# Moving the start of one filler stream in a hand-woven order: the last layer of group 6 of a four-layer graph network

## The chip, the cores and the metric

The kernel runs on one core of one Trainium2 chip. The metric is the device time of one execution in microseconds (us), from a few runs; a profile of one further execution is used to see where the time goes.

## What is computed

Thirty-two graphs `x` of 512 nodes with 256 features share one sparse 512 x 512 matrix `adj`. Four layers follow each other. Layers 0 and 3 have the same form and their own weights:

```python
pre_u = h_t @ W1[:d];  pre_v = h_t @ W1[d:]
hidden = relu(pre_u[:, :, None, :] + pre_v[:, None, :, :] + b1)
S   = sigmoid(hidden @ W2 + b2)                    # one number for each pair u, v
a_t = einsum('buv,bud->bvd', S * A_a, h_t)
m_t = einsum('uv,bud->bvd', A_m, h_t) * h_t
z_t = beta1*h_t + beta2*(a_t @ Wa + ba) + beta3*(m_t @ Wm + bm)
```

`A_a` and `A_m` are both `adj`. Layer 1 is `z + relu((adj @ z) @ W.T + b)`. Layer 2 is an attention: a softmax over `leaky_relu(f1_i + f1_j) + adj`, applied to `x @ W1.T`, plus the input. All is float32.

## The kernel before, in words

**Sparse edges.** `S` is needed only where `adj` is not zero. The kernel first turns `adj` into 36 lists of 128 edges, called items (32 for the first eight neighbours of each node, 4 for the rest). The graphs are worked on in eight groups, 0 to 7, of four entries (graphs) each. For each group and for each of layers 0 and 3, `pre` (L560) computes `pre_u` and `pre_v` of every node and writes them to a table in DRAM (`table<-puv`, L577). `edges` (L606) then goes through the 36 items. GpSimd (POOL) gathers the 128 rows of 4 KB at the other ends of the edges (L602), VectorE (DVE) adds the own rows (`mine`, L674), and relu, times W2 and a sum follow. In the last group's edges of layer 3 that is one DVE instruction of 128x1024 (L680) and four of ScalarE (ACT, L685); elsewhere it is four of DVE (L687). Every four items the sigmoid is finished (L587, L591, L592, L631). The results are put into a dense array `cells` in DRAM by an indirect write of POOL (L596). When all puts are done, `load` (L706) reads `cells` back as `SA`, four tiles of 128x2048.

**Stages.** Each group passes through these streams, each a Python generator that yields after every piece:

- `first` and `edges` of layer 0: table and edge values;
- `middle` (L773, L810): for each of the four entries, the end of layer 0, layers 1 and 2, and at the end the `pre` of layer 3. The lines that matter here are WT (L45 `WT,hT`), `adjT,zW`, L852, the projection `WT,yT`, L870, the softmax on DVE and ACT (L878 to L884), its transposes (L923) with ACT's copy `eT` (L924), the product `eT,feats`, L901, the product `w_L_gnn_W,yT` of `pre`, and the transposes L912;
- `edges` of layer 3;
- `last` (L987): the end of layer 3. For each of its four entries there are eight pieces: two of `hWa` (L45 `L_gnn_Wa,hT` with ACT's copy L725), two of `mhT` (L45 `adj,h` with DVE's product L735), two that open the sums over `SA` (L972, preceded by DVE's L965), and two that close them (L981, then DVE's L984). The output of an entry leaves by a DMA on SyncE (SP, L998 or L1007) once the next entry's `hWa` is recorded. Then the next `h` (L928) is loaded, and after `mhT` the next `hT` (L933).

The last group has no group behind it. Its last layer is cut in two: `last_before` computes `hWa` and `mhT` during the edges, and `last_behind` does the sums (L972, L981) and the outputs (L956) at the very end.

**Order.** `weave` (L444) orders all pieces by planned times in units of one group. A stream of kind "main" (the middle stages) runs at its own times. Pieces of a "fill" stream (`first` and `last`) fall due at their times; while a main stream runs up to eight (`HELD`) are held back, and one or two of them run where a main piece yields a true value, which marks places where TensorE (PE) would otherwise wait:

```python
if kind == "fill":
    due.append((k, j))
    fill(HELD if running else 0)
...
if room and due:
    fill(len(due) - (1 if len(due) < HELD // 2 else 2))
```

The times are set in `sparse_path`. For group t, `end` is the planned end of its middle stage; `last` of group t has 33 pieces, spread evenly over `behind`. For t = 6, `end` is 6.53. The middle stage of group 7 is planned from 6.53 to 7.33, its edges from 7.333 to 7.79, and `last_before` from 7.62. The framework then schedules the recorded instructions, each engine's in one fixed order, and inserts the waits. On each engine instructions run in that order; SP starts DMAs in its order too.

Of the kernel before, what the change touches and what calls it, by code (L numbers as in the profile page):

```python
# [1009 lines left out]
def even(n):  # L1010
    return [1.0] * n
# [6 lines left out]
def spread(shares, a, b):  # L1018

    times, at = [], 0.0  # L1020
    for share in shares:
        times.append(a + (b - a) * at / sum(shares))
        at += share
    return times


def edge_times(ahead, a, b, behind, lead=LEAD):

    step = (b - a) / ITEMS
    first = [ahead + j * min(step, (a - ahead) / lead) for j in range(lead)]  # L1030
    return first + spread(even(ITEMS), a, b) + spread(even(TAIL), b, behind)


def middle_shares(given):


    hWa = [] if given else [1.7, 1.7]
    shares = list(hWa)
    for b in range(NB):
        more = hWa if b < NB - 1 else []  # L1040
        shares += [] if given else [2.8, 2.8]
        shares += [3.4, 3.4, 1.0, 2.7]
        shares += [1.7, 3.4, 2.8, 4.5] + [0.9] * NC
        shares += [0.4, 0.4, 0.4, 1.0, 0.4, 1.0] + more + [1.5, 1.5]
        shares += [2.8, 4.5] + [0.4] * NC + [0.5, 0.5]
    return shares + [0.1]


@with_exitstack
def sparse_path(ctx, m, counts, xr, outr, B):  # L1050


    sp = Sparse(ctx, m, counts, xr, outr, B)
    last = B // NB - 1
    streams = [
        (sp.setup(), spread(even(NC + 1 + NC + 2 * (OWN // 2 + 1) + 1), -0.40, -0.295), ""),
        (sp.setup_behind(), spread(even(2 * (OWN // 2 + 1) + 2 * PANELS + 4), -0.285, -0.16), ""),
        (sp.setup_rest(), spread(even(7), -0.26, -0.20), ""),
        (sp.zeros_behind(), spread(even(2), 0.15, 0.2), ""),
    ]  # L1060
    for t in range(last + 1):
        g0, g3 = Group(sp, m.g0, f"0_{t}"), Group(sp, m.g3, f"3_{t}")
        start, end = (max(0.0, k - 0.47) for k in (t, t + 1))

        if t == 0:
            first = spread(FIRST, -0.385, -0.30)
            edges0 = edge_times(-0.292, -0.27, -0.03, -0.02, LEAD_AT_ENDS)
        elif t == 1:
            first = spread(FIRST, -0.28, -0.06)
            edges0 = edge_times(0.02, 0.07, start - 0.06, start - 0.04)  # L1070
        else:
            first = spread(FIRST, start - 0.86, start - 0.6)
            edges0 = edge_times(start - 0.552, start - 0.505, start - 0.06, start - 0.04)
        edges3 = edge_times(end + 0.003, end + 0.05, end + 0.48, end + 0.54)
        behind = end + 0.56, end + 1.13
        if t == last - 1:
            edges3 = edge_times(end + 0.003, end + 0.05, end + 0.46, end + 0.5)
            behind = end + 0.6, end + 1.08
        if t == last:
            end -= 0.2  # L1080
            edges3 = edge_times(end + 0.003, end + 0.02, end + 0.45, end + 0.46, LEAD_AT_ENDS)
            behind = end + 0.29, end + 0.45
        streams += [
            (sp.first(g0, t * NB), first, "fill"),
            (sp.edges(g0, ("yT", "mhT3") if t == 0 else ()), edges0, ""),
            (sp.middle(g0, g3, t * NB), spread(middle_shares(t == 0), start, end), "main"),
            (sp.edges(g3, ("yT", "h1", "hT1") if t == last else ()), edges3, "free"),
        ]
        if t == 0:
            streams.append((sp.middle_before(g0, 0), spread(AHEAD, -0.15, -0.03), ""))  # L1090
        if t < last:
            streams.append((sp.last(g3, t * NB), spread(LAST, *behind), "fill"))
        else:
            streams.append((sp.last_before(g3, t * NB), spread(AHEAD, *behind), ""))
            streams.append((sp.last_behind(g3, t * NB), spread(BEHIND, end + 0.5, end + 0.6), ""))
    sp.weave(streams)
# [191 lines left out]
@with_exitstack  # L1288
def adj_seq_kernel(ctx: ExitStack, tc: tile.TileContext, a: dict, out: bass.AP):
    nc = tc.nc  # L1290
    x = a["x"]
    B = x.shape[0]
    xr = x.rearrange("b (c p) d -> b p c d", p=P)
    outr = out.rearrange("b (c p) d -> b p c d", p=P)
    m = Model(ctx, tc, a)
    counts = Counts(ctx, m)
    excess = nc.values_load(counts.excess[0:1, 0:1])
    with tc.If(excess > 0) as branch:
        dense_path(m, xr, outr, B)
    with branch.Else():  # L1300
        sparse_path(m, counts, xr, outr, B)
# [32 lines left out]
```

## Time and profile before

| | us |
|---|---|
| median of 3 runs | 3160.87 |
| lowest and highest of them | 3154.97, 3162.56 |
| the profiled execution, its own time | 3165.21 |
| its span, first to last instruction | 3163.5 |
| PE, DVE, ACT, POOL busy in it | 2734.3, 2357.2, 977.2, 1468.5 |
| mean granted TensorE clock | 0.931 of full speed |

The profile is one execution, so times read from it are held against its own 3165.21 first and then against the median. Busy shares are means over the whole span. The change touches only its last 290 us, so the views used below are cut to stretches of that part. Times in them are us from the start of the span. A line such as L45 is a helper that issues most of the matmuls, so these are told apart by their tiles. Each float32 matmul shows as two records.

### The profile page before, as it was taken

The page shows a single profiled execution, that of the slowest core. Times are in us where ns is not written, and L with a number is a line of the kernel's source. Part 1 is how long each engine was busy: PE and PEld are TensorE (multiplying, and loading weights), DVE is VectorE, ACT ScalarE, POOL GpSimd, SP SyncE. Part 2 cuts the span into 40 slices and gives each one's busy share as a digit, 9 for nine tenths or more (in the row PEclk, how much of TensorE's full clock was granted, in tenths as well). Part 3 has the DMA queues.
Part 4 walks back from the last instruction along what each step waited for, and adds up shares of the span by engine and source line. Part 5 has one row for each costly group of instructions (what it writes and reads, how often), then busy time and mean ns, then how long its engine had stood idle before and what let it go on. Part 6 is the DMA issues. An engine that isn't in the chain of part 4 may idle for free. (4 is left out here: it accounts for less than half of the span.)

```text
span 3163.5 us, 32203 instructions
## 1 busy us (share of the span) xinstructions
PE 2734.3 (86%) x8645; PEld 1650.1 (52%) x8646; DVE 2357.2 (75%) x7594; ACT 977.2 (31%) x2309; POOL 1468.5 (46%) x1312
## 2 busy tenths in 40 slices
PE   6357878889998899989998899989998899979947
PEld 3133444446654565445654565545654466545626
DVE  6773777988589875988588785888679885872661
ACT  4453343222233222332232222332222222232440
POOL 1462453656345552546335562555435563450461
PEclk9688889999998999989998999999999899989979
DMA  8874547876667757786667766786567766551653
GB/s 290 289 231 149 167 160 234 260 246 224 210 206 256 226 191 225 232 275 201 227 191 243 244 208 206 230 268 230 184 215 249 257 212 220 178 190 47 217 189 113
DMA packets 302718, 679.38 MB, mean 215 GB/s; under 512 B 52673, under 2 KB 170945, under 8 KB 294337
## 3 DMA queue, kind: packets, MB, share of 16 engines
q0 software_dynamic: 120384, 406.01, 40.7%
q1 hardware_dynamic: 163184, 234.01, 21.9%
q10 hardware_dynamic: 18960, 37.24, 3.1%
q8 instruction: 70, 1.15, 0.1%
q14 instruction: 120, 0.98, 0.1%
HBM read 531.12 MB, written 146.01 MB: 214 GB/s over the span
## 5 line engine op out<-in xcount | busy, mean ns | idle before, releaser
L602 POOL DMA_INDIRECT rows<-table,iv x554 | 631.8, 1140 | 874.6 <-DVE rows L687 211.6
L596 POOL DMA_INDIRECT cells<-s,cell x576 | 671.1, 1165 | 625.7 <-DMA cells<-s,cell 422.4
L674 DVE TENSOR_TENSOR rows<-rows,mine 128x1024 f32<-128x1024 f32 x554 | 669.1, 1217 | 154.6 <-DMA rows<-table,iv 143.0
L687 DVE SCALAR_TENSOR_TENSOR rows<-rows,L_gnn_W2bc 128x256 f32<-128x256 f32 x2016 | 740.9, 418 | 2.1
L45 PE MATMUL pst<-adj,h 128*128 128x512 f32 x1024 | 454.6, 595 | 0.0
L45 PE MATMUL pst<-L_gnn_Wa,hT 128*128 128x256 f32 x1024 | 266.5, 413 | 123.3 <-DMA hT<-xT 53.7
L45 PEld LDWEIGHTS pst<-adj,h 128*128 128x128 f32 x1024 | 193.8, 191 | 219.0 <-issue 215.4
L45 PEld LDWEIGHTS pst<-L_gnn_Wa,hT 128*128 128x128 f32 x1024 | 209.9, 210 | 171.7 <-issue 64.1
L45 PE MATMUL pst<-w_L_gnn_W,hT 128*128 128x512 f32 x512 | 245.2, 617 | 8.4 <-ACT hT L557 6.0
L45 PE MATMUL pst<-WT,hT 128*128 128x256 f32 x512 | 166.8, 486 | 93.3 <-DVE hT L833 92.7
L45 PE MATMUL pst<-eT,feats 128*128 128x512 f32 x512 | 232.0, 607 | 10.6 <-ACT eT L924 10.0
L45 PE MATMUL pst<-w_L_gnn_W,yT 128*128 128x512 f32 x512 | 226.5, 594 | 1.0 <-DVE yT L901 1.0
L45 PE MATMUL pst<-adjT,zW 128*128 128x512 f32 x512 | 224.9, 592 | 0.0
L972 PEld LDWEIGHTS pst<-hWa,SA 128*128 128x128 f32 x896 | 212.8, 328 | 5.7 <-issue 3.3
L972 PE MATMUL pst<-hWa,SA 128*128 128x256 f32 x896 | 215.0, 397 | 0.0
L794 ACT COPY flat<-SA 128x512 f32<-128x512 f32 x128 | 136.9, 1133 | 237.8 <-PE pst L45 173.5
L825 PE MATMUL pst<-flat,hWa 128*128 128x512 f32 x448 | 196.8, 592 | 0.0
L45 PEld LDWEIGHTS pst<-WT,hT 128*128 128x128 f32 x512 | 121.8, 247 | 142.7 <-DVE hT L833 117.2
L923 PE MATMUL pst<-ident,ex 128*128 128x128 f32 x512 | 92.3, 318 | 114.5 <-DVE ex L884 63.6
L570 ACT COPY puv<-pst 128x256 f32<-128x256 f32 x256 | 93.5, 371 | 292.5 <-DVE puv L569 246.3
L569 DVE TENSOR_TENSOR puv<-pst,bc_L_gnn_b 128x256 f32<-128x256 f32 x256 | 104.2, 415 | 87.8 <-DMA table<-puv 48.0
L45 PEld LDWEIGHTS pst<-eT,feats 128*128 128x128 f32 x512 | 96.8, 193 | 127.1 <-issue 109.5
(166 smaller groups left out, 3646.2 us busy)
## 6 DMA issues: line engine op xcount, KB each, us to landing
table<-puv SPq DMA_DIRECT2D x256, 256.0 KB
SA<-cells POOLq DMA_DIRECT2D x64, 1024.0 KB
h<-in_x_dram SPq DMA_DIRECT2D x64, 512.0 KB
mine<-table SPq DMA_DIRECT2D x64, 512.0 KB
hT<-xT SPq DMA_DIRECT2D x36, 512.0 KB
h<-x2s SPq DMA_DIRECT2D x36, 512.0 KB
xT<-hT ACTq DMA_DIRECT2D x32, 512.0 KB
x2T<-yT SPq DMA_DIRECT2D x32, 512.0 KB
```

Source lines behind the costliest of these rows:

```text
L45: nc.tensor.matmul(out, lhsT, rhs, start=(n == 0), stop=(n == len(pairs) - 1))
L569: nc.vector.tensor_tensor(puv[:, 0, :], pp[:, 0:D], w["b1bc"], ALU.add)
L570: nc.scalar.copy(puv[:, 1, :], pp[:, D:])
L596: self.nc.gpsimd.indirect_dma_start(out=g.cells[half], out_offset=bass.IndirectOffsetOnAxis(ap=at, axis=0), in_=s, in_offset=None)
L602: self.nc.gpsimd.indirect_dma_start(out=rows, out_offset=None, in_=g.table, in_offset=bass.IndirectOffsetOnAxis(ap=at, axis=0))
L674: self.behind(nc.vector.tensor_tensor(rows, rows, other, ALU.add))
L687: nc.vector.scalar_tensor_tensor(part, part, 0.0, w["W2bc"], ALU.max, ALU.mult, accum_out=at)
L794: self.nc.scalar.copy(flat[:, r, :], SA[r][:, :, b])
L825: nc.tensor.matmul(pz, hWa[:, r, cs], flat[:, r, :], start=(r == 0), stop=False)
L923: nc.tensor.transpose(pt[:, js], ex[:, js], self.m.ident)
L972: nc.tensor.matmul(pz[:, k * D : (k + 1) * D], SA[r][:, cs, b], hWa[:, r, :], start=(r + k == 0), stop=False)
```

## The change

The window of `last` of group 6 (`t == last - 1`) is made shorter and begins later: from 7.13..7.61 to 7.23..7.59 in the units of the plan.

```diff
         behind = end + 0.56, end + 1.13
         if t == last - 1:
             edges3 = edge_times(end + 0.003, end + 0.05, end + 0.46, end + 0.5)
-            behind = end + 0.6, end + 1.08
+            behind = end + 0.7, end + 1.06
```

No instruction is added or removed. In the order of the plan, pieces 0 to 11 of the 33 ran before the middle stage of group 7 ended, and 12 to 14 directly at its end; now pieces 0 to 6 run before its end, and 7 to 10 directly at it. The later ones follow every 0.0109 units in place of every 0.0145, and all are still recorded before `last_before` starts.

## The prediction

> **What bounds the kernel now.** The clock per core says one core at a mean granted TensorE clock of 0.931, span 3163.5 us. The diff touches one group of eight only, so I cut the end of the run into stretches at the visible events: end of the last middle stage, first gathered row, first wait of VectorE for a row, last item, first final sum. Windows table (columns: length, then busy us and count of PE, PEld, DVE, ACT, POOL, then clock, DMA share, GB/s):
>
> ```profile
> 2876.00:2948.50 72.50, 69.82 (x234) 43.74 (x233) 22.78 (x50) 15.12 (x32) 0.00 (x0) 0.98 0.15 48
> 2948.50:2961.40 12.90, 12.90 (x58) 12.23 (x58) 1.46 (x6) 1.30 (x4) 5.78 (x7) 1.00 0.97 255
> 2961.40:3017.70 56.30, 51.66 (x184) 37.09 (x182) 56.24 (x67) 36.93 (x167) 37.58 (x28) 1.00 0.73 255
> 3017.70:3088.10 70.40, 26.24 (x64) 15.59 (x64) 42.36 (x59) 30.87 (x144) 45.69 (x38) 0.68 0.56 183
> ```
>
> In the first row PE works 69.8 of 72.5 us and POOL nothing: the last middle entry is bound by PE, and no edge can start before its table is written. In the third row DVE never rests (56.24 of 56.30); in the fourth PE is two thirds idle and DVE waits for gathers. So PE work is dear before 2948.5 and cheap after about 2962.
>
> The PE timeline shows what in that first row belongs to the last layer of group 6 (start, length, tiles, number of records, in brackets the idle time before it; each matmul has two records):
>
> ```profile
> 2820.91 3.72 PE L45 MATMUL pst<-WT,hT 128*128 128x256 f32 x16 [0.82 <-DVE hT L833]
> ...
> 2881.07 3.62 PE L45 MATMUL pst<-L_gnn_Wa,hT 128*128 128x256 f32 x16
> ...
> 2887.98 7.03 PE L45 MATMUL pst<-adj,h 128*128 128x512 f32 x16
> ...
> 2901.71 7.61 PE L972 MATMUL pst<-hWa,SA 128*128 128x256 f32 x32
> ...
> 2911.77 1.89 PE L981 MATMUL pst<-L_gnn_Wm,mhT 128*128 128x256 f32 x8
> ...
> 2914.36 1.89 PE L981 MATMUL pst<-L_gnn_Wm,mhT 128*128 128x256 f32 x8
> ...
> 2916.53 3.62 PE L45 MATMUL pst<-L_gnn_Wa,hT 128*128 128x256 f32 x16
> 2921.68 0.66 PE L923 MATMUL pst<-ident,ex 128*128 128x128 f32 x4 [1.54 <-DVE ex L884]
> ...
> 2923.24 5.29 PE L45 MATMUL pst<-adj,h 128*128 128x512 f32 x8
> ...
> 2937.11 3.60 PE L45 MATMUL pst<-adj,h 128*128 128x512 f32 x8
> ```
>
> By the start of the row that follows each, these pieces hold PE for 3.46, 6.87, 7.45, 1.72, 1.73, 3.46, 5.14 and 3.43 us: 33.3 us, from 2881.07 to the end of the middle stage at 2948.3, which I call M. They are entry 0 of that layer whole, and hWa and mhT of entry 1.
>
> Last, the waits in the edges after M, POOL's and then DVE's (engine, tile, line, released by: total us, times, longest):
>
> ```profile
> POOL cells L596 <- DMA cells<-s,cell: 19.5, 8, 5.3
> POOL rows L602 <- ACT rows L685: 7.6, 5, 2.4
> ```
>
> ```profile
> DVE rows L674 <- DMA rows<-table,iv: 14.9, 3, 10.4
> DVE rows_more L674 <- DMA rows_more<-table,iv: 9.3, 4, 4.5
> ```
>
> POOL waits for buffers (ACT L685) only from 2965 to 2977; afterwards its gathers and puts stand mostly 0.3 us apart, or behind an earlier put's landing. From about 2979 the edges run at POOL's pace.
>
> **What the Trainium skill says.** "TensorE: Matmul & The Clock Gate", section Why this matters for your kernels: a PE gap beyond about 3 us brings the clock back to half. The trace agrees: the same 16 records of hWa take 3.62 us in a busy stretch and 6.76 us at 3040.4, after 22.8 us of idle. "DMA: Bandwidth & Descriptors", section Issuing engines are not separate DMA queues: whichever engine starts them, DMAs share the same 16 engines and interleave. The trace agrees: DMA share 0.97 just after M, with SP's and POOL's transfers together. "GPSIMD Engine Reference", section Key points: it shares SBUF interfaces with VectorE instructions of two SBUF inputs. A gather (L602) takes 0.94 us beside an idle DVE and up to 1.95 beside a busy one; I read that as consistent.
>
> **The change part by part.** The instruction order of the two builds differs only from the last L832 of the last middle entry on. Nothing is added or dropped.
>
> *1. Taken out of the middle stage.* After: hWa and mhT of entry 0, both halves of its L972 and half of its L981 stay: 3.46 + 6.87 + 7.45 + 1.73 = 19.5 us. Out go half of entry 0's L981 (1.73), hWa of entry 1 (3.46) and mhT of entry 1 (5.14 + 3.43): 13.8 us. "Most of the layer" is thus a large word: before, 33.3 us of it were inside, after, 19.5.
>
> *2. What cover goes.* hWa no longer stands before WT (L45 WT,hT), so PE waits for L833, 0.82 as in the row at 2820.91. The softmax gap after L870, filled by hWa (3.46) before, is filled by half of mhT (3.43): no cost. The slow half-layer behind L923 (5.14 where 3.43 is full clock, 1.7 lost) becomes half of L972 in the same place: 1.7 lost again. Half of L972 now stands where PE waited 0.7 for ACT's eT (L924): 0.7 won. DVE's softmax has one L735 and two L965 (0.60 + 1.32) put between its links; the first transpose is not late, the last about 2 us, within the L972 that runs ahead of it. Sum: 13.8 - 0.8 - 1.7 + 0.7 = **12.0 us earlier at M**. Bounds: 10 if that DVE slip shows, 13.5 if the clock does not dip. The path from M to the first gather (table write, L577, 5.4 us) is the same.
>
> *3. What lands in the edges, on DVE.* Two L735 (0.60), two L965 (0.66) and one L984 (0.60) move past M. L984 fits in the 10.4 us wait for the first row. The rest, 2.5 us, lands in the stretch without idle. But by item 6 (of 36 in L674) both orders have done the same six such operations; only inside items 1 to 5 is the new one 0.7 to 1.9 us later, and there POOL waits for the buffers. Also the first L631 comes one item later, and POOL's first put with it. Later on POOL issues into buffers that have been free for 3 to 12 us, so delay there is absorbed. I take **+1.5**, bounds 0 and 3.
>
> *4. On PE, after M.* 1.7 + three entries of 21.2 us (3.46 + 6.87 + 7.45 + 3.44) = 65 us, where before it was 53. DVE meets the last of them (L984 of entry 3) after item 20 or 21, about 69 us after M. Slack 4 us: no cost at full clock.
>
> *5. ACT.* Two hWa copies (0.6 each) go past M, before the first item: hidden.
>
> *6. DMA and queues.* One output (L998), one h load (L928) and one hT load (L933) of 512 KB pass on SP from before M to after it; the output now waits for L984 with the two diagonal writes (L626), one mine load (L642) and the next h load behind it. L984 is ready some 2.5 us after M and that mine is needed only at item 13, so the wait is free. The 1.5 MB is not: at the 255 GB/s of the second row it is 6 us of DMA time, 4 of them (output and h) in the burst of first gathers. The first gather shares the engines as before, and the second to fifth have 1 to 3 us before DVE wants them. I take **+0.7**, bounds 0 and 2.5. POOL issues the same 76 transfers; two of its puts swap places with gathers.
>
> *7. Behind the last item* (from 3088) the last puts, the SA loads and the final sums are unchanged: nothing.
>
> Sum: -12.0 + 1.5 + 0.7 = **-9.8 us**. The profiled execution took 3165.2 (span 3163.5), 4.3 above the median 3160.9; its own forecast is 3155.4, against the median **3151**.
>
> **The rivals.** (a) *Gain given back in the first gathers.* Every bound against me: 10 at M, less 3 and 2.5, is -4.5: 3156. For it: DMA at 0.97 and DVE without idle. Against: rows that come a little late only eat DVE idle time after 3018, of which there is 28 us.
> (b) *PE becomes the bound of the edges, slower than before.* DVE and ACT run in order, so an L735 or L984 or a hWa copy that waits for PE holds the items behind it. For it: PE's hT load must wait for L735 of the entry before (2.25 us of idle at 3007 came of that), and after such gaps PE has run at half clock. Price: item 20 is 69 us after M; late PE is free up to 4 us for DVE, and POOL's buffers hide some 10 more. Beyond 14 us each further us costs one, and at 24 the 9.8 are gone. That needs 65 us of work to take 89: a mean clock of 0.73, against the 1.00 of the third row and the 0.68 of the fourth. With half clock in two of the three entries PE comes 42 us late: 42 - 14 - 9.8 = +18, 3179. Against: gaps are short while work is queued.
> (c) *The change does less than it says.* Entry 0's L972 now stands inside the softmax chain. If both its halves run at low clock there (1.7 each) and DVE's slip of 2 us shows as well, 13.8 - 0.8 - 3.4 - 2 = 7.6 go, and -5.4 is left: 3155. PE waited only 2.7 us in the whole first row, which speaks against it.
>
> **How the numbers follow.** 0.3% of 3160.9 is 9.5 us, about what a measurement of this kernel tells from no change. My sum stands just beyond that line. Forecast (-9.8; ends -13.5, and -12 + 3 + 2.5 = -6.5): 0.62, of which 0.50 beyond the line. (a) and (c): 0.26, nearly all within it. (b): 0.12, of which 0.10 over the line. So faster 0.52, same 0.37, slower 0.11. Range: -13.5 less 1 for scatter, up to zero gain: 3146 to 3161.
>
> **What would show it.** Right: PE's last L912 some 12 us earlier; between the first POOL gather and the last item 2 us more than the 134 of now; the stretch from there to the end unchanged at 75. Wrong: M less than 10 us earlier (step 2); DVE waits for PE at L735 or L984 inside the items, or ACT at hWa (step 4 and b); a first L674 later than 13.1 us after M (step 6).

## The result, and the profile after

| | before | after |
|---|---|---|
| median of 14 runs each, us | 3161.72 | 3155.51 |
| lowest and highest | 3154.16, 3166.40 | 3144.33, 3166.59 |
| profiled execution, own time (span) | 3165.21 (3163.5) | 3159.73 (3158.0) |

The ratio is 0.9975, with a 95% interval from 0.9963 to 0.9988: some 8 us faster (6 by the medians), where -9.8 was forecast. The time 3155.5 lies in the range. As a point it stays just within 0.3% of no change. So the sum came out a little too large, and the question is which of its terms did.

In us, stretches of one program repeat better than its whole time: behind the first L832 two profiles of one program differ by some 4 us at most in the table below, while the times of after lie up to 22 us apart. I cut the end of each profile at the same events: the first L832 of the last middle entry, M (end of its last L912), the first gathered row that VectorE (DVE) adds (L674), the start of the last item's L680, and the end. The second pair of profiles comes from experiments below.

| us | before | before, second | after | after, second |
|---|---|---|---|---|
| start to first L832 (same instructions in all) | 2877.6 | 2885.0 | 2879.7 | 2882.3 |
| last middle entry, L832 to M | 70.64 | 68.94 | 55.76 | 55.76 |
| M to first L674 | 13.14 | 12.78 | 15.62 | 15.48 |
| first L674 to last L680 | 120.9 | 125.0 | 124.7 | 123.9 |
| last L680 to the end | 81.2 | 82.5 | 82.3 | 83.3 |
| L832 to the end | 285.9 | 289.2 | 278.4 | 278.4 |

Means of the two columns: 69.8 to 55.8 (-14.0), 13.0 to 15.6 (+2.6), 122.9 to 124.3 (+1.4), 81.8 to 82.8 (+0.9), in all -9.1. The first row of the table shows why single times say little: the part that the change does not touch already scatters by 7 us.

The windows table of after answers to that of before, row by row (length, then busy us and count of PE, PEld, DVE, ACT, POOL, then clock, DMA share, GB/s):

```profile
2879.65:2935.42 55.77, 54.22 (x190) 34.63 (x188) 18.84 (x45) 14.18 (x30) 0.00 (x0) 1.00 0.10 33
2935.42:2951.03 15.61, 15.61 (x58) 11.28 (x57) 2.06 (x7) 2.68 (x6) 7.58 (x8) 1.00 0.97 291
2951.03:3003.20 52.17, 47.24 (x166) 36.28 (x166) 52.13 (x64) 31.98 (x145) 29.96 (x22) 0.93 0.71 245
3003.20:3075.80 72.60, 38.82 (x117) 25.87 (x116) 45.42 (x55) 32.12 (x148) 48.15 (x39) 0.76 0.60 201
```

The first row is the gain: TensorE (PE) is busy 54.2 us where it was 69.8 (that window began 1.6 us ahead of its first L832). The second row is 2.7 us longer (2.5 when both are counted from M, as in the table), and in it the DMA engines move 291 GB/s in place of 255. In the third DVE again never rests (52.13 of 52.17). In the fourth PE does 38.8 us of work where it did 26.2; some of what left the first row is here.

PE's timeline of after, in the last middle entry:

```profile
2883.08 3.87 PE L45 MATMUL pst<-WT,hT 128*128 128x256 f32 x16
...
2904.45 3.60 PE L45 MATMUL pst<-adj,h 128*128 128x512 f32 x8
2909.61 0.66 PE L923 MATMUL pst<-ident,ex 128*128 128x128 f32 x4 [1.55 <-DVE ex L884]
2910.10 4.00 PE L972 MATMUL pst<-hWa,SA 128*128 128x256 f32 x16
2913.94 1.47 PE L923 MATMUL pst<-ident,ex 128*128 128x128 f32 x12
2915.25 4.00 PE L972 MATMUL pst<-hWa,SA 128*128 128x256 f32 x16
2919.08 7.03 PE L45 MATMUL pst<-eT,feats 128*128 128x512 f32 x16
```

The softmax gap ahead of the first L923 is as before (1.55 and 1.54). Two further waits stood there before, of 0.41 ahead of its second four records and of 0.7 ahead of `eT,feats`:

```profile
2922.75 0.66 PE L923 MATMUL pst<-ident,ex 128*128 128x128 f32 x4 [0.41 <-DVE ex L884]
...
2930.14 7.13 PE L45 MATMUL pst<-eT,feats 128*128 128x512 f32 x16 [0.72 <-ACT eT L924]
```

Both are gone: L972 stands in their places. The half of L972 behind the first L923 ends after 3.84 us, at a granted clock of 1.00; the half of `adj,h` that stood there before took 5.14.

Last, the waits from M to the last item, first POOL's, then DVE's, then ACT's:

```profile
POOL rows L602 <- ACT rows L685: 13.8, 9, 5.3
POOL cells L596 <- DMA cells<-s,cell: 12.8, 5, 5.4
```

```profile
DVE rows L674 <- DMA rows<-table,iv: 20.1, 4, 12.4
```

```profile
ACT hWa L725 <- PE pst L45: 3.2, 3, 1.6
```

POOL waits for buffers 13.8 us in place of 7.6 (12.5 and 6.8 in the second profiles): the first items free them later. DVE waits 12.4 us for its first row, 10.4 before (12.3 and 10.0 in the second profiles). Neither engine waits long for PE: ACT's longest is 1.6, and DVE's waits for PE in this stretch come to 0.4 us.

### The profile page after: what moved, and what is told of

The parts are those of the page before. It is cut to its first block, busy times and chain, and to the rows that moved or that the text cites. A ratio compares the mean times of both kernels' runs of the same rounds, so it can differ in the third digit from the quotient of the medians.

```text
span 3158.0 us, 32198 instructions
## 1 busy us (share of the span) xinstructions
PE 2731.9 (87%) x8646; PEld 1649.1 (52%) x8646; DVE 2354.6 (75%) x7594; ACT 977.7 (31%) x2309; POOL 1471.3 (47%) x1312
## 4 chain that ended last, share of the span: by engine, by line
PE 44%; DVE 26%; DMA 17%; issue 7%; ACT 4%; POOL 2%; ACTq 0%; SPq 0%; POOLq 0%; DVEq 0%
PE pst L45 30%; DVE rows L687 8%; DVE rows L674 7%; PE pst L972 7%; DMA rows<-table,iv 5%; DMA table<-puv 3%; PE pst L981 3%; DMA cells<-s,cell 3%; PE pst L825 2%; PE pst L923 1%; DVE both L572 1%; DVE ex L879 1%; DMA SA<-cells 1%; DVE both L573 1%; DVE puv L569 1%
## 5 line engine op out<-in xcount | busy, mean ns | idle before, releaser
L602 POOL DMA_INDIRECT rows<-table,iv x554 | 625.2, 1128 | 861.8 <-DVE rows L687 209.5
L674 DVE TENSOR_TENSOR rows<-rows,mine 128x1024 f32<-128x1024 f32 x554 | 668.5, 1216 | 164.0 <-DMA rows<-table,iv 154.1
L972 PEld LDWEIGHTS pst<-hWa,SA 128*128 128x128 f32 x896 | 212.8, 328 | 5.7 <-issue 3.1
L972 PE MATMUL pst<-hWa,SA 128*128 128x256 f32 x896 | 215.3, 398 | 0.0
L923 PE MATMUL pst<-ident,ex 128*128 128x128 f32 x512 | 92.3, 319 | 112.1 <-DVE ex L884 50.2
```

Of the source, the lines that this page charges most:

```text
L602: self.nc.gpsimd.indirect_dma_start(out=rows, out_offset=None, in_=g.table, in_offset=bass.IndirectOffsetOnAxis(ap=at, axis=0))
L674: self.behind(nc.vector.tensor_tensor(rows, rows, other, ALU.add))
L923: nc.tensor.transpose(pt[:, js], ex[:, js], self.m.ident)
L972: nc.tensor.matmul(pz[:, k * D : (k + 1) * D], SA[r][:, cs, b], hWa[:, r, :], start=(r + k == 0), stop=False)
```

## The experiments

All edits are relative to after, unless said otherwise. "Items" is the stretch from first L674 to last L680, "tail" the one behind it. The experiments ran on three chips. Each ratio is against runs of before on the same chip (medians 3170.26, 3164.43 and 3162.83 us), so the times of two experiments are not always to be held against each other; the stretches are. An experiment with one time has no ratio, and its stretches alone are read.

**The pair again.** The after kernel, unchanged:

> The changed kernel once more, for a second profile of it. Four lengths are compared throughout: the last middle entry (L832 to the end of L912, 70.6 us before, 55.8 after), the first row (first gather of POOL to first L674: 7.6 and 10.5), the edges (first gather to the last L680: 128.5 and 135.2), the tail (last L680 to the end: 81.2 and 82.3). Theory 1, these belong to the program: 55.8, 10.5, 135.2 and 82.3 again, each within 1 us, and a time some 7 us below the kernel before. Rival, they are the scatter of one execution: at least one of the first three is off by 2 us or more towards the value of before.

Measured: 3157.94 us (14 runs), ratio 0.9962, interval 0.9948 to 0.9977. The middle was 55.76 again, to the hundredth. The rest repeated less well: the first row landed 9.2 us after the first gather in place of 10.5, and from the first gather to the last L680 it took 133.1 in place of 135.2. So the rival has a point for the edges, which were 2.1 us nearer to before. And the before kernel, unchanged:

> The kernel before once more, for a second profile. Two later lengths are kept apart from here on: M to the first L674 (13.1 before, 15.6 and 15.5 in the two profiles of the changed kernel) and the items, first L674 to last L680 (120.9 before, 124.7 and 123.9). Theory 1, all lengths belong to the program: middle entry 70.6, M to first L674 13.1, items 120.9, each within 1 us, and half of mhT behind the first L923 again takes about 5.1 us, at a low clock. Rival, the slow half of mhT and the short items are one execution's luck: middle below 69.5 or items above 122.5.

Measured: one time, 3175.88 (nine other times of before on that chip: 3160.07 to 3175.41), and the second column of the table. The rival came true on both counts. The middle is 1.7 us shorter than the first profile of the same program, and one line of PE's timeline says why:

```profile
2930.60 3.60 PE L45 MATMUL pst<-adj,h 128*128 128x512 f32 x8
```

The same eight records took 5.29 in the profile of the prediction, behind the same two waits of 1.54 and 0.41, at a granted clock of 0.67; here it was 1.00. So the low clock there comes in some executions and not in others. And the items took 125.0 where they had taken 120.9 in the same program: 4 us of scatter in that stretch, within which the moved DVE work (2.5 us) cannot be seen.

**Only the later start.**

```diff
-            behind = end + 0.7, end + 1.06
+            behind = end + 0.7, end + 1.08
```

> One part of the change alone: the window starts at end + 0.7 but still ends at end + 1.08. Theory 1, the later start does all of it: middle 56 within 1 us, M to first L674 15.5, items 124 within 1.5. Rival, the earlier end (pieces 6% closer) costs in the items what the start brings: items 122 or less.

Measured: middle 55.54, M to first row 14.38, items 125.0, tail 83.0, L832 to end 277.9; one time, 3155.07. The later start brings the whole gain in the middle, and the earlier end of the window adds nothing to it. M to the first row is 1.1 to 1.2 us shorter than in after; on SP the output stands behind both `mine` loads here and between them in after. With one profile this is not more than a hint that the earlier end costs something there.

**The output out of the burst.** The output of entry 0 and the next `h` load are recorded after the next `hT` load, and SP starts them in that order.

```diff
-            if done is not None:
+            if done is not None and b != late:
                 nc.sync.dma_start(self.outr[i + b - 1], done)
...
                 hT = self.x2T_of(i + b + 1)
+            if b == late:
+                out = nc.sync.dma_start(self.outr[i + b - 1], done)
...
+                self.tc.add_manual_dep(out.ins, self.hT_load.ins.name, order, reason="behind the load of hT")
+                ahead = self.x2_of(i + b + 1)
```

> The changed kernel, but the output of entry 0 (512 KB) and the load of h of entry 2 are held on SP until the hT load of entry 2 has been issued, some 22 us after the middle stage, so that they are out of the burst of first gathers. Theory 1, the first row is late by DMA traffic: first row back to 7.6, edges 135.2 - 3 = 132, time 3 us below the changed kernel. Rival, the filler's DVE work between the first items makes the edges longer: first row may move, but the edges stay at 134 to 136.

Windows from the first gather to the first L674, after and then this kernel:

```profile
2940.53:2951.03 10.50, 10.50 (x34) 6.77 (x33) 0.00 (x0) 0.58 (x1) 7.58 (x8) 1.00 1.01 292
```

```profile
2941.22:2948.19 6.97, 6.97 (x20) 3.77 (x19) 0.00 (x1) 0.00 (x0) 5.44 (x6) 1.00 0.99 222
```

In after SP starts the output at 2938.82, 1.7 us ahead of the first gather, and the DMA engines are full to the first row: 10.50 us at 292 GB/s, 3.1 MB. Here the output starts at 2955.33, and 1.5 MB moves in 6.97 us. M to the first L674 is 13.24, as before the change: the transfers that crossed M cost the 2.4 us. They cost it behind the first gather. From M to the first gather and from there to its row it takes 5.5 and 7.6 us in before (5.3 and 7.4 in the second profile), 5.1 and 10.5 in after (6.3 and 9.2), and 6.3 and 7.0 here.

From the first gather to the last L680 it took 132.6, as the theory had it; but the second profile of after has 133.1 without this edit. Items took 125.7, and in them DVE waited once for 5.1 us at L735 for PE, whose `mhT` of entry 2 had to wait 5.3 us for the delayed `h`. Tail 80.7, L832 to end 275.4, 3 us less than after; the timed ratio to before is 0.9959 (0.9943 to 0.9976), against 0.9962 for after on the same chip, so 3 us are not confirmed in time. And it is not the whole story: two kernels below, whose last layer of group 6 starts later still, have no output in the burst and stand at 15.18 and 14.25: 6.5 us from M to the first gather in both, then 8.7 and 7.8 to its row. Why their first gather starts later, and its row lands later than the 7.0 here, stays open.

**Filler left out of the edges.** Entries 1 to 3 of the last layer of group 6 are left out, and with them the outputs of those three graphs.

```diff
...
-        for b in range(NB):
+        for b in range(entries):
...
-            streams.append((sp.last(g3, t * NB), spread(LAST, *behind), "fill"))
+            entries = 1 if t == last - 1 else NB
+            streams.append((sp.last(g3, t * NB, entries), spread(LAST, *behind)[: 8 * entries + 1], "fill"))
...
```

> The changed kernel without entries 1 to 3 of the last layer of group 6 (their hWa, mhT, sums and outputs are left out; their graphs are not computed), with the output of entry 0 and two h loads still in the burst. It shows the edges with no filler work on PE, DVE and ACT. Theory 1, the burst holds the first row and the filler's DVE work between the first items the rest: first row still about 10, edges 130 or less. Rival, POOL's own pace sets the edges whatever DVE does: edges 134 or more.

Measured: middle 55.76, M to first row 15.99, items 116.2, tail 80.7; one time, 3146.8. With 11.2 us of DVE work, most of the PE work and the loads of three entries gone, the items are 7.7 and 8.5 us shorter than in the two profiles of after. From the first gather to the last L680 it took 126.8, where the theory had 130 or less and the rival 134 or more. That is beyond the scatter of 4: filler in the edges does cost there, though most of what is left out here lay in the edges before the change too. At that rate 2.5 us of DVE work would cost 1.7 to 1.9, an estimate; but loads and PE work went too, so the rate is not DVE's alone.

**Only L965 left out**, the six of entries 1 to 3 of group 6, so that `beta1*h + bias` is missing from three graphs:

```diff
-        for c in range(0, NC, 2):
+        for c in () if skip and b else range(0, NC, 2):
...
```

> The changed kernel without the six L965 of entries 1 to 3 of group 6 (their beta1*h + bias is left out, so their graphs come out without it). That takes 6 x 0.66 = 4.0 us of DVE work out of the edges and nothing from PE, POOL or SP. Theory 1, the filler's DVE time in the first twenty items goes into their length nearly one for one: items 124.3 - 3 = 121 or less. Rival, POOL's pace absorbs it, as the prediction had it for all but 1.5 us: items 123 to 125.

Measured: items 122.5 against 124.7 and 123.9, L832 to end 275.3; one time, 3147.06. The direction is that of the theory, but 122.5 lies between the two forecasts, and 1.8 us lie within the scatter. The price of DVE work in the edges is not settled by this run.

**The start later still.**

```diff
-            behind = end + 0.7, end + 1.06
+            behind = end + 0.8, end + 1.06
```

> The changed kernel with the filler starting at end + 0.8 in place of end + 0.7: the whole last layer of group 6 lies behind the middle stage. Theory 1, the middle is bound by PE: of the 19.5 us of filler that were still inside about 14 come out (3.4 lay in the softmax gap, some 2 covered L852 and eT), so 42 us; no output in the first burst, so first row 7.6; four entries of DVE work in the edges, 137 to 140; time about 9 us below the changed kernel. Rival b of the prediction, PE becomes the bound of the edges with 85 us of work: edges above 150, time equal to the kernel before or slower.

Measured: middle 45.34, M to first row 15.18, items 126.3, tail 90.7, L832 to end 277.6; ratio 0.9958 (0.9940 to 0.9975), the same as after. From the first gather to the last L680 it took 135.1: rival b, with more than 150, is out at this start too. The middle is now empty of filler: no `L_gnn_Wa,hT`, L972 or L981 is left between its L832 and L912. Taking out the last 19.5 us of work won 10.4, because the waits stand open again and PE runs slower behind them, as PE's timeline of this kernel shows:

```profile
2909.05 4.45 PE L923 MATMUL pst<-ident,ex 128*128 128x128 f32 x16 [5.09 <-DVE cols L883]
2914.17 9.09 PE L45 MATMUL pst<-eT,feats 128*128 128x512 f32 x16 [0.68 <-ACT eT L924]
```

In after the same 16 transposes took 0.66 and 1.47 us and `eT,feats` 7.03; here the granted clock was 0.67 from 2909.05 to 2922.7. The slower work makes up some 4.4 us and the longer waits 4.2 of the 9 that were not won.

Of the gain of 10 some 8 us are lost in the tail and 2 in the items. PE's last layers of the last group (`last_before`) are late there:

```profile
3102.59 5.32 PE L45 MATMUL pst<-L_gnn_Wa,hT 128*128 128x256 f32 x16 [8.64 <-DMA hT<-x2T]
```

This is entry 3, waiting for its `hT`. All four entries use one `hT` buffer, so each load waits until DVE, in order behind the items, has done L735 of the entry before. The last `mhT` ended at 3114.6, 20 us after the last `SA` loads were issued.

**Two buffers.** `last_before` takes `hT` and the by then unused buffer `eT` in turn; with the start at 0.8:

```diff
-    def x2T_of(self, i):
-        hT = self.act.tile([P, DC, N], F32, name="hT3", tag="hT")
+    def x2T_of(self, i, tag="hT"):
+        hT = self.act.tile([P, DC, N], F32, name="hT3", tag=tag)
...
-            h, hT = self.x2_of(i + b), self.x2T_of(i + b)
+            h, hT = self.x2_of(i + b), self.x2T_of(i + b, ("hT", "eT")[b % 2])
```

> A start at end + 0.8 as in the run before, and the hT tiles of last_before (group 7) taken in turn from two buffers (tag hT and the free tag eT), so that an hT load need not wait for L735 of the entry before. Theory 1, the tail of that run (90.8 in place of 82) was PE's late last_before: the tail goes back to 82 or less, middle 45, items 126, M to the end 223 or less, time 8 us or more below the changed kernel (about 0.993 of before). Rival, the tail was late because PE's queue as a whole is behind after four entries: tail 88 or more, time as with the start at end + 0.8 alone.

Measured: middle 45.32, M to first row 14.25, items 123.6, tail 77.0, L832 to end 260.2. Time 3138.96 (5 runs), ratio **0.9923 (0.9906 to 0.9939)**. The theory held, and the tail is not only back from 90.7 but shorter than the 81 to 83 of before and after. So the single buffer may have held the tail in those as well. The same edit on after itself:

> after with one edit: last_before loads the transposed inputs of its four entries into two buffers in turn (hT, eT) in place of one. Theory (the single hT buffer keeps PE's last_before late, and its sums over SA start only when the last mhT is done): middle 55.8, row and items as in after, tail 76 to 78 in place of 82.3 and 83.3, so L832 to end about 273 in place of 278.4. Rival (two buffers gain only with the start at 0.8, where PE's last layer comes latest, and here the SA loads that follow the puts hold the tail): tail 81 to 83, L832 to end 278.

Measured: middle 55.76, M to first row 15.70, items 122.3, tail 72.8, L832 to end 266.5; time 3140.36 (6 runs), ratio 0.9936 (0.9914 to 0.9958). The rival is out, and the theory had the gain too small. The chain of waits shows where to look (start, us, what). After, from entry 3's load on:

```profile
3081.46 4.50 DMA hT<-x2T
...
3086.09 12.31 PE pst L45 x32
...
3100.38 8.23 DMA SA<-cells
```

With two buffers:

```profile
3086.28 5.27 DMA SA<-cells
...
3091.60 9.20 PE pst L972 x28
```

In after the `hT` load and PE's last `hWa` and `mhT` are drawn as links of the chain; in the new kernel `mhT` is done at 3048, before the last item, and the chain runs through the puts straight to the `SA` loads. The link from PE to the `SA` loads is no wait, however. POOL starts the last two of them 2.64 us after the last put in after and 2.66 in the new kernel, and with the later start only they start 1.2 us before the last `mhT` is done; in the second profiles of before and after the chain comes through the puts too. So it is the puts that let the `SA` loads go in both, and what a late `mhT` costs lies beside and behind them.

The 9.5 us of tail are a sum of four. The last two `SA` loads start 23.0 us after the last L680 in place of 24.1: 1.1. From there PE has its last tile after 5.3 us in place of 8.9, with no `h` load beside the `SA` loads: 3.5. And PE, idle early, sums over the first `SA` tiles ahead, as its timeline of the new kernel shows:

```profile
3074.42 9.24 PE L972 MATMUL pst<-big,SA 128*128 128x256 f32 x28 [26.08 <-DMA SA<-cells]
```

So L972 of entries 1 to 3 is 4.83, 5.76 and 6.70 in place of 7.63 three times: 5.6. Entry 0's takes 0.7 longer (9.20 for 8.52). That the `h` load is what slows the `SA` loads was not tested alone.

It is the single buffer, and not a lack of time on PE, that makes `mhT` late. In the kernel with the filler left out PE has three entries less to do, and yet its last `mhT` ends 22.8 us after the last L680 (22.7 in after): entry 3's `hT` load starts 5.7 to 5.8 us after the last L680 in both, when DVE has done L735 of the entry before.

The same edit on before:

> before with the same edit (two buffers for last_before), windows of the change left as before. Theory (the two gains are independent and add): middle 69 to 71, tail 76 to 78, L832 to end about 282 in place of 285.9 and 289.2. Rival (the two buffers need the room that the change makes): tail 81 to 82.5 as before.

Measured: middle 68.93, M to first row 13.02, items 126.9, tail 68.5, L832 to end 277.3; time 3156.18 (18 runs), ratio 0.9983 (0.9972 to 0.9994). The tail shrinks without the change as well, by 13 to 14 us, more than the theory had. The time fell by only 0.17%, some 5 us, so part of that came back in this program's items (126.9 is the longest of all), or is scatter; I can't tell which from one profile. This kernel and the one above are also a third pair for the change itself, on one chip and with two buffers on both sides: middle -13.2, M to first row +2.7, items -4.6, tail +4.3, L832 to end -10.8.

**The start at 0.9, two buffers.**

```diff
-            behind = end + 0.8, end + 1.06
+            behind = end + 0.9, end + 1.06
```

> after with two buffers and the window of the last layer of group 6 at 0.9 to 1.06 of the plan. Theory (PE work is dear before M and cheap after it): the middle falls below the 45.3 of the start at 0.8, by at most 10 if PE has no filler left in its own waits, about 3 to 5 net of them; L832 to end 256 to 259 against 260.2 of the start at 0.8 with two buffers. Rival (the fillers that were left at 0.8 stood in waits that PE has anyway, and PE's last layers now end too late for the final sums): middle 43 to 45, tail 80 to 88, L832 to end 263 to 270.

Measured: middle 45.48, items 125.9, tail 92.9, L832 to end 278.6; time 3158.63 (12 runs), ratio 0.9984 (0.9968 to 1.0001). The middle is as the rival had it, and the tail is worse than either forecast. From the windows table, first row to the end of the last `mhT`:

```profile
2933.80:2990.00 56.20, 15.26 (x56) 13.27 (x57) 44.81 (x51) 30.59 (x146) 31.35 (x26) 0.61 0.71 253
2990.00:3059.70 69.70, 62.44 (x223) 46.93 (x222) 53.35 (x68) 33.88 (x152) 52.16 (x45) 0.98 0.70 220
3059.70:3104.10 44.40, 44.02 (x141) 26.55 (x140) 9.66 (x20) 6.69 (x17) 8.04 (x10) 1.00 0.52 190
```

PE has 15 us of work in the first 56, then 62 in 70, and from the last item on it is full without a rest for 44 us, up to 3104. This is rival (b) of the prediction in another place: PE became the bound, of the tail and not of the items.

## Why the prediction was right, step by step

- **Step 1 held.** The pieces that left, and those that stayed, are the ones named.
- **Step 2, 12.0, was too small:** 14.9 against the profile that it was made from, 13.2 against the second one and 13.2 in the pair with two buffers. WT waited 0.26 and not 0.82. The low clock of 1.7 was not "lost again": L972 in that place ran 3.84, and that dip is not in every execution of before either. L972 took the 0.7 us wait for `eT`, as said, DVE's softmax was not late, and the 0.41 wait, which I had not priced, went too. From the first profile: 13.8 - 0.26 + 0.72 + 0.41 = 14.7, for 14.9 measured. The path from M to the first gather, taken as the same, was 5.1 and 6.3 us in the two profiles of after, 5.5 and 5.3 in those of before.
- **Step 3, +1.5, is not contradicted and not shown.** The items are 1.4 longer in the mean of two pairs, with 4 us between two profiles of one program, and 4.6 shorter in the pair with two buffers. POOL's longer wait for buffers has the sign of this step, but step 6 delays the same items, and with the later start only, where the same work is moved, that wait is 6.6 us, no longer than in before. The forecast of 2 us more from the first gather to the last item came out as 3.7 in the mean of the two pairs (6.7 and 0.7).
- **Step 6, +0.7, was the other term that was mis-sized:** +2.6, just past the end of its bound. The prediction had named a first L674 later than 13.1 us after M as the sign that this step is wrong; it came 15.6 after. "The first gather shares the engines as before" was the wrong sentence. The output goes out ahead of the first gather, and the gather takes 9.2 to 10.5 us to land in place of 7.4 to 7.6; with the output and the `h` load behind it moved, it took 7.0, and the 2.4 us went away.
- **Steps 4 and 5 held.** DVE met no late PE in the items, ACT's wait was 3.2 us in all. Rival (b) did not happen at this start; at 0.9 the slack was used up.
- **Step 7, nothing, held for the change** (+0.9 in the mean, within scatter). But the reading of the tail was incomplete: "the last puts, the SA loads and the final sums" left out `last_before`, whose late `mhT` lengthens the tail in both kernels. No view that I had cut to the edges showed it; the chain of waits pointed to it, with an `hT` load at 3088.07 of before. It mattered for no number here, and it was the largest gain of those tried.

The two errors, 1 to 3 us too little gain in step 2 and 1.9 too little loss in step 6, nearly cancelled: -9.1 in the stretches for -9.8 on paper. That the sum came so close is luck; that the gain comes from the middle, and part of it is given back in the first gathers, is not. Rival (a) had the right mechanism (the gain is partly given back in the first gathers) at a smaller size; rival (c) is out, as M came even earlier than forecast.

Two versions beat both kernels, as far as ratios taken on different chips can say: two buffers alone (0.9936) and with the start at 0.8 (0.9923). The interval of the second (0.9906 to 0.9939) lies below both of after; that of the first (0.9914 to 0.9958) overlaps with the second one of after (0.9948 to 0.9977), and there the stretch from L832 to the end, 266.5 against 278.4, speaks for it. Which of the two is the better is not decided.

## What to carry to other kernels

Work that fills a bound engine's waits is worth keeping only up to those waits: here the first 13.8 us of filler that left won 13 to 15, the last 19.5 won 10.4, and past that point a later start only made the filler late. When transfers move with the work, look at which queue they enter ahead of which first gather; and before a stretch is called unchanged, follow the chain of waits through it to the end, since a single buffer reloaded in step with another engine's order can lengthen a tail though no busy share shows it. A link in that chain is a reading: check it against what the waiting instruction needs, and against a second profile.

## What was not expected of the hardware

- The Trainium skill, "TensorE: Matmul & The Clock Gate", section Why this matters for your kernels, names idle gaps beyond about 3 us as what brings the clock back to half. Here a dip stood behind waits of 1.54 and 0.41 us, in one profile of a program and not in the other (5.29 us at a granted clock of 0.67 against 3.60 at 1.00 for the same eight records).
- The middle, bound by PE, took 55.76 or 55.77 us in six profiles of kernels that share it. The items, bound by DVE and gathers, took 120.9 and 125.0 in two profiles of one program.
- From the start of the last two `SA` loads (1 MB each) PE had to wait 8.9 us for the last tile in the first profiles of after and before (8.3 and 7.6 in the second ones), and 5.1 to 5.4 in the three kernels with two buffers whose tail is short. In the former an `h` load of 512 KB is started within 3.1 us ahead of them. That they go together is seen in all seven profiles; that one causes the other was not tested alone.
